# Normalised x turned into matrix operands by transfers and a VectorE block transpose instead of TensorE transposes

## The chip, the cores and the metric

The kernel runs on one core of a Trainium2 chip. The core has TensorE (PE in the profile; its weight loads are PEld), VectorE (DVE), ScalarE (ACT), GpSimd (POOL) and SyncE (SP), which here issues every DMA. SBUF is the on-chip memory with 128 partitions, PSUM the accumulators that TensorE writes. The metric is the device time of one execution in microseconds; the time of a kernel is the median of its runs.

## The reference

The input x is 8 x 2048 x 512 in fp32. Two layers with a residual each. The second is a layer with 16 experts that take `s_len // 16` tokens each; its sequence length here is 8, so each takes none, and what is left of it is a layer norm with gain and shift. The first layer is where the change lies:

```python
x = x + _layernorm(_L0_attn_ref(_layernorm(x, axis=-1), Wq, bq, Wk, bk, Wv, bv, Wo, bo), axis=-1)
x = x + _layernorm(_L0_ffn_ref(_layernorm(x, axis=-1), ...), axis=-1)

def _L0_attn_ref(x, Wq, bq, Wk, bk, Wv, bv, Wo, bo):
    n, s, e = x.shape
    h, d = (16, 32)
    def proj(W, b):
        y = jnp.einsum('nse,fe->nsf', x, W) + b
        return y.reshape(n, s, h, d).transpose(0, 2, 1, 3)
    Q, K, V = proj(Wq, bq), proj(Wk, bk), proj(Wv, bv)
    scores = jnp.einsum('nqhd,nkhd->nhqk', Q, K) * scale
    attn = jax.nn.softmax(scores, axis=-1)
    out = jnp.einsum('nhql,nlhd->nqhd', attn, V)
    out = out.reshape(n, s, e)
    return jnp.einsum('nse,fe->nsf', out, Wo) + bo
```

`proj` hands over (n, head, position, d), and the einsums name the second axis q, k or l and the third h: for every token this is attention among its own 16 heads. The result, with the head outermost, is reshaped straight into rows.

## The kernel before

**Tiling.** The 16,384 tokens are cut into 32 units of 512 tokens, and a unit into four tiles of 128. A unit goes through four steps, c = 0 to 3. Everything is fp32 and the order of all instructions is written out by hand (`manual_schedule`): each engine, and the SP queue, runs its instructions in the order in which the program issues them.

**What a step holds.** `STEPS[c]` is a string of items that `step` walks through. While step (u, c) does the softmax and the weighing of unit u, it also computes part of the products for Q, K and V of unit u + 1 (items such as `q1`, `k5`, with `e` for the copy out of PSUM and `w` for the write to a DRAM scratch), the output product and row work of unit u - 1 (`d1` to `d7`, `ra` to `re`), and prepares the x tile s + 8 or s + 9, where s = 4u + c. The products use Strassen's scheme: seven products of quarters (`multiply`, line 317) instead of eight, so x is needed also as sums and differences of its quarters.

**The path of an x tile before the change.** `load_x` (line 243) loads tile s + 11 in step s (item `lx`), one token per partition. `stat_x` and `norm_x` (items `xs`, `xn`, tile s + 9; lines 183, 190, 191, 260, 261) subtract the mean and multiply by the inverse deviation on VectorE, with the inverse root on POOL, and POOL's memset puts a 1 in the last column (for the biases). One step later, for tile s + 8, `turn_x` (item `px`, line 267) turns the tile with four 128 x 128 TensorE transposes into one PSUM bank, so that features lie on partitions. `keep_x` (item `xa`, lines 279 and 281) copies it with ACT into `xb`, the operands of a unit (seven quarter blocks of 2 x 256 columns). For the tiles 2 and 3 of a unit `add_x` (item `xt`) makes t3 and t1 on VectorE (lines 290, 291; one source is the PSUM bank) and t2 and t4 on POOL (lines 292, 293).

Feature `128*ec + p` lies in chunk ec on partition p, and the weights for Q, K and V are loaded in the same order (`load_weight`, line 139, `"(ec p) f -> p ec f"`).

**TensorE around it.** In steps 1, 2 and 3 `px` stands at the end of the step, ahead of the scores of the next step (`sc`, line 393) and the weighing of this one (`av`, line 442). In step 0 it stands at the beginning, ahead of the product `q1` (tile `paq`).

**SP.** In the order of the items: x and r loads (`lx`, `lr`), writes of Q, K and V to DRAM (lines 364, 367; `qs<-cq`, `ks<-ck`, `vs<-cv`), their spreads back in another layout (`sq`, `sk`: line 376, `qd<-qs`, `kx<-ks`; `sv`: line 382, `vd<-vs`) and stores of finished rows (`st`, line 589). A DMA that has to wait for its data holds up those behind it. `kx` and `vd` have one buffer each. Step 2 ends in `k3w sc av` and step 3 begins with `sk lx lr`; the scores that need that `kx` are issued at the end of step 3.

**VectorE and the softmax.** Each step begins its softmax with `mx` (lines 404, 406: the maximum and the subtraction), then ACT's exp (414), the sum and reciprocal (419, 420), POOL's product (421), a VectorE block transpose of 32 x 32 blocks (426), and four ACT copies into `ex` (431), which the weighing reads.

**The start.** `first_unit` prepares tiles 0 to 7, all weights and the products of unit 0 in an order of its own; `FIRST_STEPS` replaces `STEPS` in unit 0. The last two units have no x tiles left to prepare.

Of the kernel before, what the change touches and what calls it, by code (L numbers as in the profile page):

```python
# [34 lines left out]
F32 = mybir.dt.float32  # L35
BF16 = mybir.dt.bfloat16
AF = mybir.ActivationFunctionType
ALU = mybir.AluOpType
# [12 lines left out]
def head_attention_norms(  # L51
# [15 lines left out]
    nc = tc.nc  # L67
    NB, S, E = x.shape
    P = 128
    H, D = 16, 32  # L70
    assert NB // H == 0, "experts that take tokens"
    EC = E // P
    Q4 = 4
# [3 lines left out]
    NT = Q4 * NU  # L77
    SCALE = 1.0 / D**0.5

    const = ctx.enter_context(tc.tile_pool(name="const", bufs=1))  # L80
    xpool = ctx.enter_context(tc.tile_pool(name="xpool", bufs=4))
    pool2 = ctx.enter_context(tc.tile_pool(name="pool2", bufs=2))
    epool = ctx.enter_context(tc.tile_pool(name="epool", bufs=2))
    dpool = ctx.enter_context(tc.tile_pool(name="dpool", bufs=4))
# [4 lines left out]
    ps_pj = ctx.enter_context(tc.tile_pool(name="ps_pj", bufs=4, space=PSUM))  # L89


    ident = const.tile([P, P], F32, name="ident")
# [43 lines left out]

    def load_weight(name, src, last=False):
        weights[name] = w = const.tile([P, EC, E], F32, name="w" + name)
        src = src.rearrange("(ec p) f -> p ec f", p=P)
        if not last:  # L140
            nc.sync.dma_start(w, src)
            return
        sums[name] = epool.tile([P, E], F32, tag="cc", name="last" + name, bufs=6)
        nc.sync.dma_start(sums[name], src[P - 1 : P, EC - 1, :].to_broadcast([P, E]))
        for i in range(2):
            nc.sync.dma_start(w[:, 2 * i : 2 * i + 2, :], src[:, 2 * i : 2 * i + 2, :])
# [27 lines left out]
    def load_row(name, b):  # L174
        t = const.tile([P, E], F32, name="r" + name)
        nc.sync.dma_start(t, b.unsqueeze(0).to_broadcast([P, E]))
        row_const[name] = t
# [59 lines left out]
    xs, xrs, xb, px = {}, {}, {}, {}  # L237

    def load_x(t):
        if t < NT:  # L240
            xs[t] = xpool.tile([P, E], F32, tag="x", name=f"x_{t}")
            n, s = divmod(P * t, S)
            nc.sync.dma_start(xs[t], x[n, s : s + P, :] if t < NT - Q4 else renumbered[t % Q4])

    def renumber(J):

# [3 lines left out]
    renumbered = dram.tile([Q4, P, E], F32, tag="xr", name="xr", bufs=1)  # L250

    def stat_x(t):
        if t < NT:
            mv = moments(xs[t], f"x{t}")
            xrs[t] = mv, rsqrt(mv[:, 1:2], f"x{t}", 1.0, EPS)

    def norm_x(t):
        if t < NT:
            mv, rs = xrs.pop(t)
            nc.vector.tensor_scalar(xs[t], xs[t], mv[:, 0:1], rs, ALU.subtract, ALU.mult)  # L260
            nc.gpsimd.memset(xs[t][:, E - 1 : E], 1.0)

    def turn_x(t):
        if t < NT:
            px[t] = ps_pj.tile([P, EC, P], F32, tag="pj", name=f"px_{t}")
            for ec in range(EC):
                nc.tensor.transpose(px[t][:, ec, :], xs[t][:, ec * P : (ec + 1) * P], ident)  # L267
            del xs[t]

    def keep_x(t):  # L270

        if t < NT:
            u, J = divmod(t, Q4)
            if J == 0:
                xb[u] = pool2.tile([P, 7, 2, 2 * P], F32, tag="xb", name=f"xb_{u}")
            j = slice(P * (J % 2), P * (J % 2) + P)
            if J < 2:
                dst = xb[u][:, 0:2].rearrange("p n e t -> p (n e) t")[:, :, j]
                nc.scalar.copy(dst, px[t])
            else:  # L280
                nc.scalar.copy(xb[u][:, 2, :, j], px[t][:, 2:4])  # L281

    def add_x(t):

        if t < NT and t % Q4 >= 2:
            u, J = divmod(t, Q4)
            j = slice(P * (J % 2), P * (J % 2) + P)
            b11, b21, b22, t1, t2, t3, t4 = (xb[u][:, n, :, j] for n in range(7))
            b12 = px[t][:, 0:2]
            nc.vector.tensor_tensor(t3, b22, b12, ALU.subtract)  # L290
            nc.vector.tensor_tensor(t1, b12, b11, ALU.subtract)
            nc.gpsimd.tensor_tensor(t2, b22, t1, ALU.subtract)
            nc.gpsimd.tensor_tensor(t4, b21, t2, ALU.subtract)

# [5 lines left out]
    def multiply(u, name, n):  # L300
        if n == 1:
            banks[name, "a"] = ps_a.tile([P, E], F32, tag="pa", name=f"pa{name}_{u}")
        elif n in (2, 5):
            banks[name, n] = ps_pj.tile([P, E], F32, tag="pj", name=f"p{name}{n}_{u}")
        ps = banks[name, {2: 2, 5: 5, 3: 5}.get(n, "a")]
        w, t = weights[name], sums[name]
        lo, hi = slice(0, 256), slice(256, 512)
        left = {
            1: w[:, 0:2, lo], 2: w[:, 2:4, lo], 3: w[:, 0:2, hi], 4: w[:, 2:4, hi],
            5: t[:, 0], 6: t[:, 1], 7: t[:, 2],  # L310
        }[n]
        right = xb[u][:, {1: 0, 2: 1, 3: 2, 4: 6, 5: 3, 6: 4, 7: 5}[n]]
        if name == "v":
            left, right = right, left
        for m in range(2):
            for e in range(2):
                nc.tensor.matmul(  # L317
                    ps[:, 256 * m : 256 * m + 256],
                    lhsT=left[:, e, P * m : P * m + P], rhs=right[:, e, :],
                    start=(n in (1, 2, 5) and m == 0 and e == 0), stop=(e == 1), skip_group_check=True,  # L320
                )
# [275 lines left out]
    def first_unit():  # L597
# [12 lines left out]
        stat_x(0)  # L610
        stat_x(1)
        norm_x(0)
        turn_x(0)
        keep_x(0)
        stat_x(2)
        norm_x(1)
        turn_x(1)
        keep_x(1)
        stat_x(3)
        norm_x(2)  # L620
        turn_x(2)
        keep_x(2)
        norm_x(3)
        turn_x(3)
        keep_x(3)
        for t in range(4, 8):
            load_x(t)
        load_weight("v", wvT, True)
# [18 lines left out]
        add_weights("k", nc.vector, (1,))  # L647
        run(0, "q3 k6 k6e q4w q5w q3e k2e")
        norm_x(4)
        stat_x(5)  # L650
        add_weights("v", nc.gpsimd)
        run(0, "q3w")
        spread_qk(0, "q")
        run(0, "k2w k5 k7 k7e v1 v1e k4 k5e k4e")
        norm_x(5)
        run(0, "k3 k4w k5w k3e k3w")
        spread_qk(0, "k")
        stat_x(6)
        run(0, "v2 v2e v2w v6 v6e")
        turn_x(4)  # L660
        keep_x(4)
        norm_x(6)
        turn_x(5)
        stat_x(7)
        load_x(8)
        run(0, "v7 v7e")
        keep_x(5)
        load_x(9)
        norm_x(7)
        turn_x(6)  # L670
        keep_x(6)
        load_x(10)
        add_x(6)
        turn_x(7)
        keep_x(7)
        run(0, "v5 v4 v5e v4e v4w v5w")
        stat_x(8)
        add_x(7)
        run(0, "v3 v3e v3w")
        scores(0, 0)  # L680
        norm_x(8)

    def run(u, items):

        for item in items.split():
            f = {"": multiply, "e": collect, "w": write}.get(item[2:])
            if f:
                f(u, item[0], int(item[1]))
# [1 line left out]


    STEPS = (
        "lx lr sv st ok sB px mx xa q1 q1e ra d2 ou dn d2e rv d6 d6e tr d5 x0 x1 x2 x3 d7 d7e rg rf q2 rt d5e xs"
        " d4 q2e re xn d4e d3 d3e rs q2w st sc av",
        "lx lr q6 q6e mx ra dn ok ou q5 rv q7 tr q7e x0 x1 x2 x3 k1 rg rf q5e k1e rt q4 xs q3 q4e re k2 q3e xn"
        " q5w q4w rs px st xa q3w k2e sc av",
        "lx lr k6 k6e mx ra dn ok ou k5 rv k7 tr k7e k2w x0 x1 x2 x3 v1 sq rg k5e rf v1e rt k4 xs k4e k5w k3 re xn"
        " k3e k4w rs px st xa xt k3w sc av",
        "sk lx lr v2 mx v2e ra v6 ok v6e dn ou ds v5 rv sA v7 tr x0 x1 v7e x2 x3 d1 rg rf v5e v2w d1e v4 rt xs"
        " v4e v5w v3 re xn v3e v4w rs px xa xt v3w sc av",  # L700
    )

    FIRST_STEPS = (
        "lx sv mx q1 q1e dn ok ou q2 q2e q6 q6e tr k1 k1e x0 x1 x2 x3 q7 q7e q2w lb xs q5 q5e xn q4 q4e px q5w q4w lo"
        " xa sc av",
        "lx k2 mx k2e dn ok ou c4 q3 tr k6 k6e x0 x1 x2 x3 q3e k2w q3w k5 xs cs k7 k7e c0 k5e xn px k5w xa sc av",
        "lx mx v1 v1e dn ok ou k4 k4e k3 k3e tr k4w k3w sq c1 v2 x0 x1 x2 x3 v2e xs c2 c3 v6 v6e xn wt px xa xt v2w sc av",
        "sk lx ds v7 v7e mx v5 v5e dn ok ou xs tr v4 v4e xn x0 x1 x2 x3 d1 sA v4w v5w d1e px v3 v3e xa xt v3w lg sc av",
    )
    stores = []  # L710

    def step(u, c):
        s = Q4 * u + c
# [7 lines left out]
        def keep_last():  # L721
# [6 lines left out]
            "x0": lambda: soft_place(0), "x1": lambda: soft_place(1),  # L728
            "x2": lambda: soft_place(2), "x3": lambda: soft_place(3),
            "av": lambda: weigh(u, c), "ok": keep_last, "ou": lay_under, "sq": lambda: spread_qk(u + 1, "q"), "sk": lambda: spread_qk(u + 1, "k"), "st": store,  # L730
            "xs": lambda: stat_x(s + 9), "xn": lambda: norm_x(s + 9), "px": lambda: turn_x(s + 8),
            "lb": lambda: load_row("o", bo), "lo": lambda: load_weight("o", woT), "lg": load_gains,
            "c0": lambda: centre_output(0), "c1": lambda: centre_output(1), "c2": lambda: centre_output(2),
            "c3": lambda: centre_output(3), "c4": lambda: centre_output(Q4), "cs": split_bias, "wt": add_output,
            "xa": lambda: keep_x(s + 8), "xt": lambda: add_x(s + 8),
        }
        of_last = {
            "ra": lambda: rows_add(*d), "rv": lambda: rows_var(*d), "rg": lambda: rows_gain(*d),
# [139 lines left out]
```

## Time and profile before

| what | value |
| --- | --- |
| median of 3 runs | 1885.67 us (1885.27 to 1886.52) |
| span of the profiled execution, first to last instruction | 1882.1 us |
| DMA packets, bytes | 370,051 packets, 312.58 MB |
| q1 hardware queue, share of the 16 engines' span | 63.0% |
| transposes of x on PE (line 267) | 512, 281 ns mean |
| copies px to xb on ACT (lines 279, 281) | 64 of 595 ns and 64 of 503 ns mean |
| subtractions on VectorE (lines 290, 291) | 64 of 417 ns and 64 of 423 ns mean |
| a unit (four steps) | 57.2 us |

The time of the profiled execution itself is not recorded apart from its span; the median of the runs is 3.6 us longer than the span. A group line of the profile gives the line of the program, the engine, the operation, what it writes and reads with shapes, how often, then the busy time, the mean duration in ns, and the idle time of the engine just before such instructions with what ended it.

### The profile page before, as it was taken

To read this page: it belongs to the slowest core of one execution; us is meant where nothing else is said; L and a number is where in the kernel's file an instruction comes from. 1 tells how busy PE (TensorE), PEld (TensorE's weight loads), DVE (VectorE), ACT (ScalarE), POOL (GpSimd) and SP (SyncE) were. 2 spreads that over 40 slices of the span, in tenths; PEclk is the share of its full clock that TensorE was granted. 3 is DMA by queue.
4 is the path that set the end of the run, shared out by engine and by line. 5 is a ranking of instruction groups with operands and counts; after the bars stand their busy time and mean duration, and the time that the engine had idled before them with its cause. 6 is when DMAs were issued, how large, how long until landed. Compare 5 with 4: busy or idle time off the path is not lost.

```text
span 1882.1 us, 57927 instructions
## 1 busy us (share of the span) xinstructions
PE 1847.4 (98%) x24026; PEld 1596.9 (85%) x24026; DVE 1423.8 (76%) x2634; ACT 1172.4 (62%) x1910; POOL 1028.9 (55%) x1785
## 2 busy tenths in 40 slices
PE   8999999999999999999999999999999999999994
PEld 7888888888888888888888888888888888888872
DVE  7667777777777777777777777777777777777777
ACT  2556566666666665666666666566666656666666
POOL 5345654555554565555556545555545555455546
PEclk9999999999999999999999999999999999999998
DMA  7765766566766657665667665576556677656671
GB/s 218 187 158 154 186 174 162 152 167 166 181 169 161 166 147 191 175 162 150 171 157 185 172 163 161 154 181 180 161 158 168 157 189 193 165 147 163 154 186 57
DMA packets 370051, 312.58 MB, mean 166 GB/s; under 512 B 149750, under 2 KB 280825, under 8 KB 365564
## 3 DMA queue, kind: packets, MB, share of 16 engines
q1 hardware_dynamic: 369788, 308.89, 63.0%
q8 instruction: 188, 3.08, 0.7%
q14 instruction: 75, 0.61, 0.1%
HBM read 174.59 MB, written 135.27 MB: 165 GB/s over the span
## 4 chain that ended last, share of the span: by engine, by line
PE 93%; POOL 2%; DVE 1%; ACT 1%; DMA 1%; issue 1%; SPq 0%; POOLq 0%; ACTq 0%; DVEq 0%
PE paq L317 12%; PE pak L317 12%; PE pav L317 11%; PE pad L507 11%; PE pk L317 9%; PE pq L317 9%; PE pv L317 9%; PE pd L507 8%; PE sa L393 6%; PE sa L442 4%; PE px L267 3%; ACT ex L431 1%; POOL rs_d L191 1%; POOL e L421 0%; POOL rs_d L190 0%
## 5 line engine op out<-in xcount | busy, mean ns | idle before, releaser
L431 ACT COPY ex<-eT 32x512 f32<-32x512 f32 x512 | 315.5, 616 | 40.1 <-DVE eT L426 31.2
L421 POOL TENSOR_TENSOR e<-e,den 128x512 f32<-128x512 f32 x128 | 134.6, 1052 | 323.2 <-DVE den L420 265.4
L191 POOL TENSOR_TENSOR rs_d<-rs_d,nhalf 128x1 f32<-128x1 f32 x384 | 211.1, 550 | 32.0
L588 POOL TENSOR_TENSOR a<-a,r 128x512 f32<-128x512 f32 x120 | 181.7, 1514 | 44.1 <-ACT a L584 27.0
L190 POOL TENSOR_SCALAR rs_d<-mv_d 128x1 f32<-128x1 f32 x250 | 50.1, 200 | 255.9 <-DVE mv_d L184 242.8
L404 DVE TENSOR_REDUCE top<-sa 128x16 f32<-128x512 f32 x128 | 88.7, 693 | 103.5 <-PE sa L442 66.7
L584 ACT ACTIVATE a<-a,nm,rs_d 128x512 f32<-128x512 f32 x120 | 97.7, 814 | 97.2 <-DVE nm L577 97.2
L414 ACT ACTIVATE e<-e 128x512 f32<-128x512 f32 x128 | 80.8, 631 | 122.7 <-DVE e L406 122.5
L453 ACT COPY oT<-sa 128x512 f32<-128x512 f32 x124 | 134.4, 1084 | 31.8 <-PE sa L442 29.6
L260 DVE TENSOR_SCALAR x<-x,mv_x,rs_x 128x512 f32<-128x512 f32 x128 | 94.7, 740 | 53.5 <-POOL rs_x L191 52.8
L419 DVE TENSOR_REDUCE den<-e 128x16 f32<-128x512 f32 x128 | 87.2, 681 | 62.9 <-ACT e L414 62.8
L393 PEld LDWEIGHTS sa<-kx,qd 64*32 64x32 f32 x8192 | 109.2, 139 | 29.9 <-issue 27.7
L133 ACT COPY sa<-under 128x1024 f32<-128x1024 f32 x129 | 131.7, 1021 | 2.1
L426 DVE STREAM_TRANSPOSE eT<-e 128x512 f32<-128x512 f32 x128 | 91.0, 711 | 54.7 <-POOL e L421 54.7
L393 PE MATMUL sa<-kx,qd 64*32 64x64 f32 x8192 | 129.1, 249 | 1.0 <-DMA vs<-cv 0.9
L543 ACT ACTIVATE junk<-a 128x512 f32<-128x512 f32 x120 | 84.1, 701 | 71.7 <-DVE a L521 71.7
L442 PE MATMUL sa<-ex,vd 64*32 64x64 f32 x8192 | 123.2, 226 | 3.9 <-ACT ex L431 3.4
L317 PE MATMUL paq<-xb,sq 128*128 128x256 f32 x512 | 124.2, 386 | 0.1
L317 PE MATMUL pak<-xb,sk 128*128 128x256 f32 x512 | 124.2, 386 | 0.0
L317 PE MATMUL pv<-wv,xb 128*128 128x256 f32 x512 | 124.1, 385 | 0.0
L317 PE MATMUL paq<-xb,wq 128*128 128x256 f32 x512 | 123.2, 384 | 0.7 <-ACT xb L281 0.4
L317 PE MATMUL pav<-wv,xb 128*128 128x256 f32 x512 | 121.2, 380 | 1.0 <-ACT u3v L337 1.0
(163 smaller groups left out, 4719.8 us busy)
## 6 DMA issues: line engine op xcount, KB each, us to landing
qs<-cq SPq DMA_DIRECT2D x128, 256.0 KB, 2.3
qd<-qs SPq DMA_DIRECT2D x128, 256.0 KB, 5.3
ks<-ck SPq DMA_DIRECT2D x128, 256.0 KB, 2.4
kx<-ks SPq DMA_DIRECT2D x128, 256.0 KB, 4.3
vs<-cv SPq DMA_DIRECT2D x128, 256.0 KB, 3.1
vd<-vs SPq DMA_DIRECT2D x128, 256.0 KB, 4.4
r<-in_x_dram SPq DMA_DIRECT2D x128, 256.0 KB, 4.9
x<-in_x_dram SPq DMA_DIRECT2D x124, 256.0 KB, 4.5
```

The lines of the kernel that those rows point to most:

```text
L133: nc.scalar.copy(sa, under.unsqueeze(1).to_broadcast([P, 2, UT]))
L191: nc.gpsimd.tensor_tensor(rs, rs, nhalf, ALU.pow)
L260: nc.vector.tensor_scalar(xs[t], xs[t], mv[:, 0:1], rs, ALU.subtract, ALU.mult)
L317: nc.tensor.matmul(ps[:, 256 * m : 256 * m + 256], lhsT=left[:, e, P * m : P * m + P], rhs=right[:, e, :], start=(n in (1, 2, 5) and m == ...
L393: nc.tensor.matmul(sa[32 * i : 32 * i + 32, t, 64 * rh : 64 * rh + 64], lhsT=qd[u][d].rearrange("p h (b m) -> p (h b) m", b=2)[:, :, m], r ...
L421: nc.gpsimd.tensor_tensor(e, e, den.unsqueeze(2).to_broadcast([P, 16, 32]), ALU.mult)
L431: nc.scalar.copy(ex[q, :, i % 2, :], sm["t"][q])
L442: nc.tensor.matmul(o[:, J], lhsT=vd[u][d, 4 * c + rh, J, :], rhs=ex[d, 8 * (J // 2) + 2 * rh + J % 2].rearrange("p i k -> p (i k)"), start ...
L453: nc.scalar.copy(dst, sa[:, :, 256:].rearrange("p t (k h R) -> p t k h R", k=Q4, h=Q4))
L507: nc.tensor.matmul(ps[:, m], lhsT=left[:, e, P * m : P * m + P], rhs=right[:, e], start=(n in (2, 5) and m == 0 and e == 0), stop=(e == 1) ...
L584: nc.scalar.activation(a, a, AF.Identity, bias=nm, scale=rs)
L588: engine.tensor_tensor(a, a, res.pop((u, k)), ALU.add)
```

## The change

Tiles 0 to 3 are turned on TensorE as before, but with a stride of four, so that chunk k holds the features 4p + k. From tile 4 on another path is taken:

- `load_x` loads a tile so that partition 4t + b holds token 32b + t.
- `move_x` (new item `xm`, tile s + 9, near the end of the step) issues four SBUF-to-SBUF transfers on SP. Transfer a takes columns 128a to 128a + 127 of all 128 partitions and lays them into the 32 partitions from 32a on: partition 32a + t then holds, for b = 0 to 3, the 128 columns of token 32b + t.
- `turn_x` (item `px`, now one place ahead of `xn`) is one VectorE transpose of 32 x 32 blocks that reads the moved tile with a stride of four elements and writes the operands in `xb` directly. The item `xa`, ACT's copy, is gone.
- `add_x` reads its third quarter from `xb` and writes t1 over it; the numbers of the blocks change accordingly.
- The weights for Q, K and V are loaded with their rows in order 4p + k.
- `xpool` has five buffers instead of four, `mpool` (two buffers) is new, and `dynamic_dma_scratch_size` is set to 1024.

```diff
-    xpool = ctx.enter_context(tc.tile_pool(name="xpool", bufs=4))
+    xpool = ctx.enter_context(tc.tile_pool(name="xpool", bufs=5))
+    mpool = ctx.enter_context(tc.tile_pool(name="mpool", bufs=2))
...
-        src = src.rearrange("(ec p) f -> p ec f", p=P)
+        src = src.rearrange("(p ec) f -> p ec f" if last else "(ec p) f -> p ec f", p=P)
...
-            nc.sync.dma_start(xs[t], x[n, s : s + P, :] if t < NT - Q4 else renumbered[t % Q4])
+            src = x[n, s : s + P, :] if t < NT - Q4 else renumbered[t % Q4]
+            nc.sync.dma_start(xs[t], src if t < Q4 else src.rearrange("(b t) e -> t b e", b=Q4))
...
+    def begin_x(t):
+        u, J = divmod(t, Q4)
+        if J == 0:
+            xb[u] = pool2.tile([P, 7, 2, 2 * P], F32, tag="xb", name=f"xb_{u}")
+        j = slice(P * (J % 2), P * (J % 2) + P)
+        n = 0 if J < 2 else 2
+        return xb[u][:, n : n + 2].rearrange("p n e t -> p (n e) t")[:, :, j]
+
+    def turn_first(t):
+        px[t] = ps_pj.tile([P, EC, P], F32, tag="pj", name=f"px_{t}")
+        for ec in range(EC):
+            part = xs[t].rearrange("p (e k) -> p k e", k=EC)[:, ec]
+            nc.tensor.transpose(px[t][:, ec, :], part, ident)
+        del xs[t]
+
+    def keep_first(t):
+        nc.scalar.copy(begin_x(t), px.pop(t))
+
+    def move_x(t):
+
+        if t < NT:
+            px[t] = mpool.tile([P, Q4, P], F32, tag="xm", name=f"xm_{t}")
+            for a in range(Q4):
+                nc.sync.dma_start(px[t][32 * a : 32 * a + 32], xs[t][:, P * a : P * a + P])
+            del xs[t]
+
     def turn_x(t):
+
         if t < NT:
-            px[t] = ps_pj.tile([P, EC, P], F32, tag="pj", name=f"px_{t}")
-            for ec in range(EC):
-                nc.tensor.transpose(px[t][:, ec, :], xs[t][:, ec * P : (ec + 1) * P], ident)
-            del xs[t]
-
-    def keep_x(t):
...
+            dst = begin_x(t).rearrange("p k (b t) -> p k b t", b=Q4)
+            nc.vector.transpose(dst, px.pop(t).rearrange("p b (e k) -> p k b e", k=EC))
...
-            b11, b21, b22, t1, t2, t3, t4 = (xb[u][:, n, :, j] for n in range(7))
-            b12 = px[t][:, 0:2]
-            nc.vector.tensor_tensor(t3, b22, b12, ALU.subtract)
-            nc.vector.tensor_tensor(t1, b12, b11, ALU.subtract)
+            b11, b21, t1, b22, t2, t3, t4 = (xb[u][:, n, :, j] for n in range(7))
+            nc.vector.tensor_tensor(t3, b22, t1, ALU.subtract)
+            nc.vector.tensor_tensor(t1, t1, b11, ALU.subtract)
...
-        right = xb[u][:, {1: 0, 2: 1, 3: 2, 4: 6, 5: 3, 6: 4, 7: 5}[n]]
+        right = xb[u][:, {1: 0, 2: 1, 3: 3, 4: 6, 5: 2, 6: 4, 7: 5}[n]]
...
     STEPS = (
-        "lx lr sv st ok sB px mx xa q1 q1e ra d2 ou dn d2e rv d6 d6e tr d5 x0 x1 x2 x3 d7 d7e rg rf q2 rt d5e xs"
-        " d4 q2e re xn d4e d3 d3e rs q2w st sc av",
-        "lx lr q6 q6e mx ra dn ok ou q5 rv q7 tr q7e x0 x1 x2 x3 k1 rg rf q5e k1e rt q4 xs q3 q4e re k2 q3e xn"
-        " q5w q4w rs px st xa q3w k2e sc av",
-        "lx lr k6 k6e mx ra dn ok ou k5 rv k7 tr k7e k2w x0 x1 x2 x3 v1 sq rg k5e rf v1e rt k4 xs k4e k5w k3 re xn"
-        " k3e k4w rs px st xa xt k3w sc av",
+        "lx lr sv st ok sB mx q1 q1e ra d2 ou dn d2e rv d6 d6e tr d5 x0 x1 x2 x3 d7 d7e rg rf q2 rt d5e xs"
+        " d4 q2e re px xn d4e d3 d3e rs q2w st xm sc av",
+        "lx lr q6 q6e mx ra dn ok ou q5 rv q7 tr q7e x0 x1 x2 x3 k1 rg rf q5e k1e rt q4 xs q3 q4e re k2 q3e px xn"
+        " q5w q4w rs st q3w xm k2e sc av",
+        "lx lr k6 k6e mx ra dn ok ou k5 rv k7 tr k7e k2w x0 x1 x2 x3 v1 sq rg k5e rf v1e rt k4 xs k4e k5w k3 re px xn"
+        " k3e k4w rs xt st k3w xm sc av",
         "sk lx lr v2 mx v2e ra v6 ok v6e dn ou ds v5 rv sA v7 tr x0 x1 v7e x2 x3 d1 rg rf v5e v2w d1e v4 rt xs"
-        " v4e v5w v3 re xn v3e v4w rs px xa xt v3w sc av",
+        " v4e v5w v3 re px xn v3e v4w rs xt v3w xm sc av",
     )
...
-    nc = _bacc.Bacc("TRN2", target_bir_lowering=False, num_devices=1)
+    nc = _bacc.Bacc("TRN2", target_bir_lowering=False, num_devices=1, dynamic_dma_scratch_size=1024)
```

In `first_unit` and `FIRST_STEPS` the items move in the same way: `turn_first` and `keep_first` for tiles 0 to 3, `move_x` after `norm_x` for tiles 4 to 8, `turn_x` where the TensorE transposes of tiles 4 to 7 stood or a little later.

## Prediction

> **What bounds the kernel.** I read the page first: busy time, the slices, the chain that ended last. Then the busy time by stage, then the chain in order of time over one unit.
>
> ```profile
> span 1882.1 us, 57927 instructions
> ...
> PE 1847.4 (98%) x24026; PEld 1596.9 (85%) x24026; DVE 1423.8 (76%) x2634; ACT 1172.4 (62%) x1910; POOL 1028.9 (55%) x1785
> ...
> PEclk9999999999999999999999999999999999999998
> ...
> PE 93%; POOL 2%; DVE 1%; ACT 1%; DMA 1%; issue 1%; SPq 0%; POOLq 0%; ACTq 0%; DVEq 0%
> ```
>
> ```profile
> 900.00:1300.00 400.00, 399.97 (x5262) 349.79 (x5261) 307.21 (x574) 254.25 (x413) 220.62 (x385) 1.00 0.64 167
> ```
>
> In the second fence (busy PE, PEld, DVE, ACT, POOL, then clock, DMA share, GB/s) PE is busy 399.97 of 400 us, at the full granted clock, and nothing interrupts it. Between 100 and 1700 us, 28 units of 57.2 us, it is busy 1598.11 of 1600. So work taken off PE shortens the span, as long as nothing else becomes late.
>
> **What the transposes cost PE.** Their own durations (281 ns x 512 = 144 us) overlap, so I take the chain's steps instead (start, length, what):
>
> ```profile
> 905.78 0.59 PE px L267 x4
> 906.37 1.73 PE paq L317 x8
> ...
> 918.48 1.73 PE pd L507 x8
> 920.20 0.89 PE sa L393 x50
> 921.10 0.71 PE sa L442 x46
> 921.81 1.92 PE paq L317 x8
> ...
> 932.37 1.73 PE pk L317 x8
> 934.09 0.44 PE px L267 x4
> 934.53 0.88 PE sa L393 x52
> ```
>
> Steps 1, 2 and 3 of a unit have four transposes ahead of the scores: 0.44 us, and the scores take 0.88 with them or 0.89 without. In step 0 they stand behind the weighing: 0.59 us, but the product behind them takes 1.73 instead of 1.92, so they are worth 0.40. A unit: 3 x 0.44 + 0.40 = 1.72 us. Tiles 8 to 127 fill 30 units: **51.6 us**. The first unit's tiles 4 to 7 take 2 x 0.87 = 1.7 us in the chain; I count these apart below. If the next instructions did not speed up or slow down at all, the bound above is 0.53 us a tile (start of the first transpose at 933.93 to the scores at 934.46): 120 x 0.53 + 1.7 = 65 us.
>
> **ACT.** 124 copies of px go (about half of 595 ns, half of 503): some 68 us off an engine at 62%. It is not the bound, so it is worth nothing by itself.
>
> **VectorE.** Added per tile: one block transpose. The trace has one of the same size.
>
> ```profile
> L404 DVE TENSOR_REDUCE top<-sa 128x16 f32<-128x512 f32 x128 | 88.7, 693 | 103.5 <-PE sa L442 66.7
> L260 DVE TENSOR_SCALAR x<-x,mv_x,rs_x 128x512 f32<-128x512 f32 x128 | 94.7, 740 | 53.5 <-POOL rs_x L191 52.8
> L426 DVE STREAM_TRANSPOSE eT<-e 128x512 f32<-128x512 f32 x128 | 91.0, 711 | 54.7 <-POOL e L421 54.7
> L453 ACT COPY oT<-sa 128x512 f32<-128x512 f32 x124 | 134.4, 1084 | 31.8 <-PE sa L442 29.6
> ```
>
> L426 reads and writes in order: 0.71 us is the lower bound. The new one reads every fourth element. No VectorE row does that; the nearest is L453, an ACT copy that writes every eighth element and takes 1084 ns where in-order ACT copies of that size (L331) take 585, 1.85 times. 0.711 x 1.85 = 1.32 us is the upper bound; adding the same 0.50 us gives 1.21. Against it, VectorE's write of every second element (ck, L353, 684 ns) costs no more than one in order (cq, 683). I take 1.2. The Trainium skill, Vector Engine (DVE) Microarchitecture Reference, section Measured stream behaviour on trn2, says that a stream runs at full rate only in runs of two adjacent words, and lists 1.73 to 2.5 ns per column where every element hops. By it the transpose would take about 1.1 to 1.5 us, an estimate from 512 columns and the page's two prices, and the sum below would hardly move; the ck row, whose hop of one word is free, doesn't follow that rule.
>
> The two subtractions of add_x now read SBUF twice instead of SBUF and PSUM. Nearest are L552 and L566, SBUF alone: 0.74 us as a rule and 1.03 when a POOL add runs beside them. Half as wide, that is 0 to 0.15 us each, four per unit; I take 0.14, so 0.56. (Once, in the start, an SBUF add beside POOL took 2.73 us instead of 0.69; that is the bound above, 1.0 us each.)
>
> Is there room? Between 100 and 1700 us VectorE waits, per unit, 3.30 us for the scores ahead of L404 (58.2 + 34.1 over 28), 0.95 for pd, 0.56 for pq, 0.47 for pv: 5.28 us in which it stands early for PE. Another 1.78 (49.9 over 28) is spent ahead of norm_x's subtraction for POOL's rsqrt, and the new transpose is issued just before that, so it fills this gap. Need: 4 x 1.2 + 0.56 + 1.72 (PE is sooner) - 1.78 = 5.3 us. So the early arrival is just used up. Behind it stand 2.01 us of waits for ACT's exp and 0.82 for ACT's copy, part of which shrink when VectorE is later, and in every step ex is ready 2 to 4 us before the weighing takes it (step 2: 944.93, weighing from 947.7). I cost it at nothing; without the early arrival, 5.36 - 1.78 = 3.6 us a unit, 107 us in 30, would be on the path.
>
> **SP and DMA.** 124 x 4 = 496 issues of 64 KB. Issues of the spreads take 0.43 us, so 1.7 us per tile; SP waits 1080 of the 1600 us, so it has the time. The order matters.
>
> ```profile
> 949.66 1.14 SPq L367 DMA_DIRECT2D ks<-ck  x1
> 950.90 3.19 SPq L376 DMA_DIRECT2D kx<-ks  x4
> ```
>
> The tightest place: in step 2 the last write of K (949.66), then now the move, then the spread of K that the scores at 961.4 need. Two of the four spreads wait for that write to land anyway (34.7 us over 28 units, 1.24 us each; qs and ks land in 2.3). The move's 1.7 us mostly fill that. Its packets (512, each 512 bytes, like qs<-cq) cost 16 engines 51 ns a packet on the mean (63.0% of 16 x 1882.1 us over 369,788): 1.6 us. The last spread lands at 953.7 + 4.2 = 957.9; with PE sooner by two transposes' 0.88 the scores want it at 960.5. Slack 2.6 us, needed 0.5 + 1.6 = 2.1. What waits behind the move on SP otherwise (loads for one and two steps on, the spread of V, which lands at 914.3 for a weighing at 920.2) has 4 us or more. The move waits for norm_x and the POOL memset, for which SP's store before it already waits (L589 on x L261, 123 us in the stage). The moved tile has 8 to 10 us until its transpose; spreads land in 8.9 at the worst. In all DMA rises from 63% by about 11 points (63,488 packets x 51 ns over 16 engines, 203 us). x's rows fetched in another order cost what r's scattered rows do (4.9 us to landing, against 4.5), two steps ahead of use. A fifth x buffer makes up for a tile that is held until its move has landed instead of until PE has read it.
>
> The trap in the Trainium skill that speaks against this: VectorE: DVE Perf Modes, The three transpose paths, calls a plain strided DMA 19 times slower than the crossbar path (1309 ns), so about 25 us a block by estimate. It holds for a large stride in the innermost dimension; here 512-byte runs move, as in qs<-cq (2.3 us). By the rule each step would wait some 15 us for its tile (25 less the 8 to 10 above), 1800 us over 120 steps, and the sum would be above 3600. No run here shows the rule.
>
> **Start.** Scores and weighing of unit 0 hang on V's last part (cv ends 52.9, vs, vd lands 61.9). Tile 7's transpose and the subtractions now stand ahead of it on VectorE, with the wait for the move: about +0.8; one move and a load then stand ahead of the spread: +0.9. The end of that chain comes 1.7 us later, and the 1.7 us saved on PE there are lost too: -1.7 net. Tiles 0 to 3 stay on PE, read with a stride: weight loads with a stride (L393) take 139 ns, in order (L442) 106, so 16 x 0.03 = 0.5 us at most, taken as 0. q, k and v weights come in another row order, in longer pieces, and wait as little as before. dynamic_dma_scratch_size: POOL issues no DMA here, nothing. The last eight steps and the last unit have no x work.
>
> **Sum.** 51.6 - 1.7 = 49.9; 1882.1 - 49.9 = 1832.2 of span. The runs' median is 3.6 above the span: **1835.8, say 1836 us**.
>
> **Rivals.**
> - *Full gain* (forecast, 0.58): at most the 65 us of the upper PE price, at least 40 (a third of a microsecond of late scores per unit): 1821 to 1846.
> - *VectorE becomes the bound* (0.18): transpose 1.32 us, subtractions 0.4 each: 5.28 + 1.6 + 1.72 - 1.78 = 6.8 against 5.28; 1.5 us a unit, 46 us in 30, so 1882. Half of it is taken up by ACT's waits: 1859. For: 76% becomes 86%. Against: the 2.8 us of other waits.
> - *K arrives late* (slower, 0.19): SP's order. If none of the move's issue hides (+1.7), its packets take twice as long in the stretch where the DMA share is already 1.0 (+3.2), and the transpose delays the last K sum by 0.5: 5.4 against 2.6 us of slack, 2.8 a unit, 84 us in 30: 1836 + 84 = 1920. It decides from 1.7 us late per unit on. For: DMA is full from 952 to 962 us. Against: the landing wait already there.
> - *The transposes were hidden*, or what PE saves is lost again at the next wait (0.05): 1885. Against: PE 93% of the chain, px 3% by name.
>
> **From this**: about 0.2% (4 us) is what can be told from no change. Faster 0.58 + 0.18 = 0.76, same 0.05, slower 0.19. The range holds the first two, up to where VectorE takes nearly all: 1821 to 1884; the forecast's own is 1821 to 1846.
>
> **What would show it.** Right: px gone from PE after 12 us, scores following a product directly, units of 55.5 us, PE still over 399 of 400, L426-like transposes near 1.2 us, the wait before L404 near zero. Wrong: idle PE ahead of L393 released by a kx or ks DMA (K late) or ahead of L442 by ex (VectorE late); transposes over 1.6 us; a move that lands over 8 us after issue.

## Result and profile after

| | before | after |
|---|---|---|
| median of the runs (us) | 1885.47 (1883.57 to 1886.52, 4 runs) | **1928.8** (1924.4 to 1929.94, 4 runs) |
| profiled span (us) | 1882.1 | 1922.6 |
| unit, most frequent length (us) | 57.21 | 58.33 |
| start of unit 1 on TensorE (us) | 104.27 | 111.33 |

The ratio is 1.0227, with a 95% interval of 1.0213 to 1.0242. The changed kernel is 2.3% slower; 1836 us were forecast, and the result lies outside the range.

From the page of the changed kernel, the busy times, the chain that ended last and three groups of instructions:

```profile
span 1922.6 us, 57824 instructions
...
PE 1821.5 (95%) x23530; PEld 1535.4 (80%) x23530; DVE 1602.6 (83%) x2758; ACT 1122.4 (58%) x1786; POOL 1035.2 (54%) x1785
...
PE 47%; DVE 14%; DMA 12%; POOL 12%; issue 7%; SPq 5%; ACT 3%; DVEq 0%; POOLq 0%; ACTq 0%
...
L295 DVE STREAM_TRANSPOSE xb<-xm 128x512 f32<-128x512 f32 x124 | 160.2, 1292 | 7.4 <-DMA xm<-x 6.3
L520 PE MATMUL pad<-so,oS 128*128 128x256 f32 x480 | 120.9, 385 | 42.0 <-POOL oS L490 42.0
...
L262 DVE TENSOR_SCALAR x<-x,mv_x,rs_x 128x512 f32<-128x512 f32 x128 | 143.5, 1121 | 1.8 <-POOL rs_x L192 1.1
```

The chain fell from 93% TensorE to 47%, and VectorE and POOL have 14% and 12% of it. TensorE now waits for POOL ahead of the output product `pad` (the row's third part: 42.0 us, put down to `oS`); before, that wait was 0.2 us. norm_x (L262, before L260) lost its wait of 52.8 us for POOL's inverse root, but its own busy time rose from 94.7 to 143.5 us. The new transposes take 1292 ns. The same stretch as before, by stage (busy PE, PEld, DVE, ACT, POOL, then clock, DMA share, GB/s):

```profile
900.00:1300.00 400.00, 386.40 (x4996) 328.97 (x4995) 341.92 (x590) 238.50 (x376) 218.83 (x377) 1.00 0.70 183
```

TensorE, busy 399.97 of 400 us before, now idles 13.6; its clock is still 1.00.

**One wait, followed back.** The timeline of one change from step 3 to step 0 in the changed kernel (start, length, engine, what), first VectorE, then POOL, then TensorE:

```profile
924.69 1.52 DVE L295 STREAM_TRANSPOSE xb<-xm 128x512 f32<-128x512 f32 x1
926.15 1.33 DVE L262 TENSOR_SCALAR x<-x,mv_x,rs_x 128x512 f32<-128x512 f32 x1
927.39 0.68 DVE L366 TENSOR_TENSOR cv<-pv,u2v 128x512 f32<-128x512 f32 x1
928.00 0.41 DVE L303 TENSOR_TENSOR xb<-xb 128x256 f32<-128x256 f32 x1
928.44 0.42 DVE L304 TENSOR_TENSOR xb<-xb 128x256 f32<-128x256 f32 x1
```

```profile
925.92 1.27 POOL L601 TENSOR_TENSOR a<-a,r 128x512 f32<-128x512 f32 x1 [0.54 <-ACT a L597]
...
928.95 0.72 POOL L305 TENSOR_TENSOR xb<-xb 128x256 f32<-128x256 f32 x1
929.75 0.73 POOL L306 TENSOR_TENSOR xb<-xb 128x256 f32<-128x256 f32 x1
930.43 1.17 POOL L489 TENSOR_TENSOR oS<-oT 128x256 f32<-128x256 f32 x1
931.68 0.72 POOL L490 TENSOR_TENSOR oS<-oS,oT 128x256 f32<-128x256 f32 x1
```

```profile
930.06 0.59 PE L520 MATMUL pad<-so,oS 128*128 128x256 f32 x2
932.46 1.56 PE L520 MATMUL pad<-so,oS 128*128 128x256 f32 x6 [1.81 <-POOL oS L490]
```

The same place in the kernel before, VectorE and POOL:

```profile
903.71 0.55 DVE L260 TENSOR_SCALAR x<-x,mv_x,rs_x 128x512 f32<-128x512 f32 x1 [0.75 <-POOL rs_x L191]
...
905.35 0.42 DVE L291 TENSOR_TENSOR xb<-px,xb 128x256 f32<-128x256 f32 x1
```

```profile
903.89 1.79 POOL L588 TENSOR_TENSOR a<-a,r 128x512 f32<-128x512 f32 x1 [0.21 <-ACT a L584]
...
906.59 0.73 POOL L292 TENSOR_TENSOR xb<-xb 128x256 f32<-128x256 f32 x1
907.40 0.72 POOL L293 TENSOR_TENSOR xb<-xb 128x256 f32<-128x256 f32 x1
908.09 0.73 POOL L476 TENSOR_TENSOR oS<-oT 128x256 f32<-128x256 f32 x1
908.89 1.06 POOL L477 TENSOR_TENSOR oS<-oS,oT 128x256 f32<-128x256 f32 x1
```

In both, POOL makes t2 and t4 of x (L305 and L306, before L292 and L293) ahead of the sums of the weighed values `oS` (L489 and L490, before L476 and L477), and `pad` needs the second of these. The product `pd` before it starts at 907.93 before and at 928.33 after. Measured from there, VectorE's last subtraction ends 2.2 us early before (905.77) and 0.5 us late after (928.86), a loss of 2.7 us; POOL's `oS` is done at +2.0 before (909.95), just as `pad` takes it, and at +4.1 after (932.40). From this come the 1.81 us for which TensorE stands. The transpose of 1.52 us and norm_x's 1.33 are where VectorE loses the time. Norm_x meets POOL's add of `a` in both kernels. Before, norm_x begins first (903.71) and takes 0.55 us, and the add (903.89) takes 1.79. After, the add begins first (925.92) and takes 1.27, and norm_x (926.15) takes 1.33. POOL's own queue is late as well: t2 (L305) starts 0.09 us after the last subtraction and 0.14 after POOL's instruction before it, where in the kernel before add_x had been ready for 0.8 us when POOL came to t2.

### The profile page after: what moved, and what is told of

It is laid out like the page before. It is cut to its first block, busy times and chain, and to the rows that moved or that the text cites. A ratio compares the mean times of both kernels' runs of the same rounds, so it can differ in the third digit from the quotient of the medians.

```text
span 1922.6 us, 57824 instructions
## 1 busy us (share of the span) xinstructions
PE 1821.5 (95%) x23530; PEld 1535.4 (80%) x23530; DVE 1602.6 (83%) x2758; ACT 1122.4 (58%) x1786; POOL 1035.2 (54%) x1785
## 4 chain that ended last, share of the span: by engine, by line
PE 47%; DVE 14%; DMA 12%; POOL 12%; issue 7%; SPq 5%; ACT 3%; DVEq 0%; POOLq 0%; ACTq 0%
PE paq L330 9%; PE pq L330 8%; PE pad L520 8%; PE pak L330 6%; PE pd L520 6%; DMA r<-in_x_dram 4%; DVE x L262 4%; DMA qd<-qs 4%; PE pk L330 3%; PE sa L406 3%; PE sa L455 2%; POOL oS L489 2%; SPq L288 2%; POOL oS L490 2%; SPq L389 2%
## 5 line engine op out<-in xcount | busy, mean ns | idle before, releaser
L192 POOL TENSOR_TENSOR rs_d<-rs_d,nhalf 128x1 f32<-128x1 f32 x384 | 226.8, 591 | 32.0
L601 POOL TENSOR_TENSOR a<-a,r 128x512 f32<-128x512 f32 x120 | 161.8, 1348 | 52.8 <-ACT a L597 52.8
L597 ACT ACTIVATE a<-a,nm,rs_d 128x512 f32<-128x512 f32 x120 | 106.2, 885 | 110.5 <-DVE nm L590 110.5
L295 DVE STREAM_TRANSPOSE xb<-xm 128x512 f32<-128x512 f32 x124 | 160.2, 1292 | 7.4 <-DMA xm<-x 6.3
L520 PE MATMUL pad<-so,oS 128*128 128x256 f32 x480 | 120.9, 385 | 42.0 <-POOL oS L490 42.0
L262 DVE TENSOR_SCALAR x<-x,mv_x,rs_x 128x512 f32<-128x512 f32 x128 | 143.5, 1121 | 1.8 <-POOL rs_x L192 1.1
L520 PEld LDWEIGHTS pad<-so,oS 128*128 128x128 f32 x480 | 88.9, 190 | 64.2 <-POOL oS L490 53.3
L330 PE MATMUL paq<-xb,wq 128*128 128x256 f32 x512 | 127.3, 392 | 2.6 <-issue 1.6
```

The costliest lines, as they stand in the source:

```text
L192: nc.gpsimd.tensor_tensor(rs, rs, nhalf, ALU.pow)
L295: nc.vector.transpose(dst, px.pop(t).rearrange("p b (e k) -> p k b e", k=EC))
L330: nc.tensor.matmul(ps[:, 256 * m : 256 * m + 256], lhsT=left[:, e, P * m : P * m + P], rhs=right[:, e, :], start=(n in (1, 2, 5) and m == ...
L520: nc.tensor.matmul(ps[:, m], lhsT=left[:, e, P * m : P * m + P], rhs=right[:, e], start=(n in (2, 5) and m == 0 and e == 0), stop=(e == 1) ...
L601: engine.tensor_tensor(a, a, res.pop((u, k)), ALU.add)
```

## Experiments

Theory A is the chain just read: VectorE has too much to do ahead of add_x, POOL's queue stands behind add_x, and `pad` behind that. Theory B is that the transfers cost the time. Times are medians beside the kernel before on the same chip (1884.3 to 1886.6). PE idle is what is missing to 1600 us of busy TensorE between 100 and 1700 us of the profiled execution; it shows only part of what the units lose (28 units of the changed kernel take 75 us more than 28 of e10, but PE idle is 53 us more). e1 to e7 ran once each, e9 to e11 twice, e8 four times and e12 five times. The runs of one kernel lie up to 5.5 us apart for the changed kernel and 11.3 us for e12, so a few microseconds between single runs tell nothing. e2, e9 and e10 leave the transfers out and so compute another output; they are there for their time alone.

| run | time (us) | unit, most frequent (mean) | PE idle |
|---|---|---|---|
| before | 1885.47 | 57.21 | 1.9 |
| after | 1928.8 | 58.33 (58.38) | 58.7 |
| e1 before + transfers | 1898.26 | 57.21 (57.75) | 10.1 |
| e2 after, no transfers | 1915.53 | 58.30 | 55.9 |
| e3 features in order | 1904.51 | (57.53) | 43.4 |
| e4 late sums | 1879.08 | 56.4 (56.82) | 21.2 |
| e5 norm_x first | 1915.92 | 57.7 (58.07) | 51.6 |
| e6 in order + late sums | 1873.64 | (56.67) | 25.4 |
| e7 late sums + start on TensorE | 1881.19 | 56.4 (57.10) | 22.8 |
| e8 all three | 1866.8 | 55.5 to 56.5 (56.57) | 21.7 |
| e9 late sums, no transfers | 1861.59 | 56.4 (56.38) | 8.6 |
| e10 all three, no transfers | 1841.15 | 55.5 (55.71) | 5.6 |
| e11 before + extra transpose | 1918.73 | 58.4 (58.45) | 24.0 |
| e12 e8, K's spread first | **1846.09** | 55.5 (55.84) | 10.2 |

**Transfers or VectorE (e1, e2).** e1 adds the four transfers per tile to the kernel before, from unit 1 on, at their new places, into a tile that nobody reads. e2 takes them out of the changed kernel.

```diff
 e1, on the kernel before
+            xm = mpool.tile([P, Q4, P], F32, tag="xm", name=f"xm_{t}")
+            for a in range(Q4):
+                nc.sync.dma_start(xm[32 * a : 32 * a + 32], xs[t][:, P * a : P * a + P])
 e2, on the kernel after
-            px[t] = mpool.tile([P, Q4, P], F32, tag="xm", name=f"xm_{t}")
-            for a in range(Q4):
-                nc.sync.dma_start(px[t][32 * a : 32 * a + 32], xs[t][:, P * a : P * a + P])
-            del xs[t]
+            px[t] = xs.pop(t).rearrange("p (b e) -> p b e", b=Q4)
```

> The kernel before, with TensorE's transposes, to which only the four transfers per tile are added on SP at the changed kernel's places, into a tile that nobody reads. Theory A (VectorE has too much to do in steps 2 and 3, add_x is late, POOL's sums for the output product are late, TensorE waits 1.8 us in step 0): no change, 1882 to 1892 us. Theory B (the transfers hold up K's spread or other DMAs): 1905 us or more, TensorE idle ahead of the scores with a DMA as releaser.

> The changed kernel without the four transfers: the block transpose reads the normalised tile itself, so tokens and features of the operands are mixed up and the output is another one. Theory A: as the changed kernel, 1915 to 1932 us. Theory B: the transfers were what held it up, 1850 us or less.

e1 took 1898.26 us, some 12 more than before and between the two expectations: half of the units keep 57.2 us, and the others take up to 61. e2 took 1915.53, in A's range: without any transfer nearly all of the loss is still there, and with it the wait (the groups of the page of e2):

```profile
L517 PE MATMUL pad<-so,oS 128*128 128x256 f32 x480 | 121.2, 385 | 51.3 <-POOL oS L487 51.3
```

So the regular 58.3 us per unit don't come from the transfers; what they cost by themselves is smaller: irregular delays in e1, and in the changed kernel mostly the start (unit 1 begins at 104.43 us in e2, at 111.33 with the transfers).

**The stride (e3).** Features go in order (chunk a, then k, then 32 in a row), so that the transpose reads runs of 32 elements; the weights' rows follow, loaded in four pieces of 32 partitions.

```diff
-            nc.vector.transpose(dst, px.pop(t).rearrange("p b (e k) -> p k b e", k=EC))
+            nc.vector.transpose(dst, px.pop(t).rearrange("p b (k e) -> p k b e", k=EC))
```

> The changed kernel with features in order 128a + 32k + e, so that the block transpose reads its source in runs of 32 elements instead of every fourth; the weights' rows are loaded to match, and tiles 0 to 3 are normalised into that order. The transpose should take 0.7 to 0.9 us instead of 1.29. Theory A: VectorE gains about 2 us a unit, 1.2 to 1.6 of it in steps 2 and 3, so 36 to 48 us less than 1929: 1880 to 1893 us. Theory B: 1925 to 1932 us.

1904.51 us: 24 better than the changed kernel, but A asked for 1880 to 1893. The groups of the page of e3:

```profile
L526 PE MATMUL pad<-so,oS 128*128 128x256 f32 x480 | 119.7, 384 | 18.2 <-POOL oS L496 18.0
L301 DVE STREAM_TRANSPOSE xb<-xm 128x512 f32<-128x512 f32 x124 | 90.5, 730 | 10.3 <-DMA xm<-x 8.9 <-DMA r<-in_x_dram 0.4
...
L267 DVE TENSOR_SCALAR x<-x,mv_x,rs_x 128x512 f32<-128x512 f32 x124 | 81.2, 655 | 2.6 <-POOL rs_x L192 1.8
L309 DVE TENSOR_TENSOR xb<-xb 128x256 f32<-128x256 f32 x64 | 58.0, 906 | 0.0
```

The transpose falls from 1292 to 730 ns and norm_x from 1121 to 655, and the wait for `oS` is more than halved. But now it is add_x's first subtraction (L309, 906 ns against some 0.42 us before) that meets POOL's add. And unit 1 starts at 117.7 us, 6.4 later than in the changed kernel, which I put down to the weights, loaded in pieces (e6, where they load as before the change, begins unit 1 at 111.2).

**The queue on POOL (e4).** For the unit's last tile, t2 and t4 are taken out of POOL's queue ahead of `oS` and put behind the product of the softmax in the next step.

```diff
+            if late and t % Q4 == 3:
+                return
+    def add_rest(t):
...
             nc.gpsimd.tensor_tensor(t2, b22, t1, ALU.subtract)
             nc.gpsimd.tensor_tensor(t4, b21, t2, ALU.subtract)
...
-" d2e rv d6 d6e tr"
+" d2e rv d6 d6e xp tr"
```

> The changed kernel with POOL's two subtractions (t2, t4) of a unit's last tile put behind the softmax's product in the next step 0, so that POOL's sums for the output product do not stand behind add_x. Theory A with the POOL queue as the path: TensorE's 1.8 us wait per unit goes, 45 to 54 us less: 1875 to 1885 us. Theory A with VectorE itself as the bound whatever POOL does: the wait turns up elsewhere, 1905 to 1930 us. Theory B: unchanged, 1925 to 1932 us.

1879.08 us, as A expected: VectorE works as slowly as before (transposes 1286 ns, norm_x 1138), and yet 50 us are gone. The group of the page of e4 that had waited 42.0 us:

```profile
L530 PE MATMUL pad<-so,oS 128*128 128x256 f32 x480 | 113.4, 379 | 0.0
```

Two POOL instructions in another place settle what the path was. The kernel is now faster than the one before, by some 7 us in its one run.

**The filled gap (e5).** norm_x ahead of the transpose again.

```diff
-re px xn
+re xn px
```

> The changed kernel with norm_x's subtraction again ahead of the block transpose (items xn px instead of px xn). In the changed kernel the subtraction comes 1.3 us later than before, meets POOL's add L601 and takes 1.18 us instead of 0.75. If that meeting is what eats the gap that the transpose was to fill: the subtraction goes back to 0.7 to 0.8 us, VectorE's wait for rsqrt (about 0.4 us a tile) comes back, and the time stays within 8 us of 1929. If the order was well chosen: 10 us or more slower than 1929. If the meeting costs more than the gap: 1905 to 1918 us.

1915.92 us, 13 less than the changed kernel, as the third case of the expectation has it. The groups of the page of e5:

```profile
L295 DVE STREAM_TRANSPOSE xb<-xm 128x512 f32<-128x512 f32 x124 | 145.2, 1171 | 6.0 <-DMA xm<-x 6.0
...
L262 DVE TENSOR_SCALAR x<-x,mv_x,rs_x 128x512 f32<-128x512 f32 x128 | 102.5, 801 | 53.6 <-POOL rs_x L192 52.9 <-POOL x L263 0.7
```

The gap of 52.9 us is back, and the kernel is faster with it: norm_x takes 102.5 us instead of 143.5, and the transposes 145.2 instead of 160.2. Between 100 and 1700 us norm_x meets POOL's add of `a` about as often as in the changed kernel, but in 54 meetings it begins ahead of the add (0.71 us on the mean) and only in 27 behind it (1.31). In the changed kernel it begins behind the add in all 80 (1.42).

**Parts put together (e6 to e8).** e6 is late sums and features in order, with the weights' rows put in order ahead of the launch, so that they load as before the change; e7 late sums with tiles 4 to 7 of the start on TensorE; e8 all three.

> Both the in-order block transpose (0.73 us) and the late POOL sums; the rows of the Q, K and V weights are put into the order 128a + 32k + e ahead of the launch, so that they load as in the kernel before. Theory A: VectorE is no longer late, a unit takes 55.5 to 56.0 us against 58.4 (changed) and 57.2 (before), 28 units: 34 to 48 us less than before, 7 of it lost in the start: 1845 to 1860 us. If something else of the change holds the steps (SP's order, the DMA load): units stay at 56.4 or more, 1872 to 1885 us.

> The late POOL sums (stride kept), and tiles 4 to 7 turned on TensorE as in the kernel before, so that the start has no transfers but tile 8's. If the transfers on SP's queue are what makes unit 1 begin 7.1 us later than before (111.3 against 104.3 us): unit 1 begins at 104 to 106 us and the time is 5 to 8 us below 1879. If VectorE's new work in the start is the cause: no change from 1879.

> In-order transpose, late POOL sums and TensorE for tiles 4 to 7 together. Theory A: what the prediction forecast, since VectorE then needs 0.56 us less per tile: units of 55.5 to 55.9 us, unit 1 from 105 us: 1838 to 1850 us. Theory B: 1870 us or more.

1873.64, 1881.19 and 1866.8 us (e8 against before: 0.99, interval 0.9878 to 0.9922). A's ranges for e6 and e8 were missed, by 14 and 17 us; e6 is in the other theory's, e8 in neither. e7 and e8 begin unit 1 at 105.4 and 105.9 us instead of 111.3, so the start's loss is found. They take both the transfers and VectorE's transposes out of the start; that it was the transfers follows from e2 (104.43), which keeps these transposes. In e7's total, for which 5 to 8 us less than e4 had been expected, nothing of it shows; e8 is 7 us below e6's one run. The shortest units of e6 and e8 are the 55.5 us that were forecast, but others take up to 60. That irregular part had to be explained.

**What is irregular (e9, e10).** e4 and e8 without the transfers, with e2's edit.

> Late sums (e4, 1879.1 us) without the four transfers per tile; the transpose reads the x tile itself, so tokens and features are mixed. Theory S: the stalls of PE that come irregularly, with no releaser in the profile, come from the transfers; then the units take e4's most frequent 56.4 us throughout instead of its mean of 56.8, and PE idles under 10 us between 100 and 1700 instead of 21: 1879 - 28 x 0.42 = 1867, so 1862 to 1870. Rival: they come from the late sums or the order of VectorE's work; then e4's time, 1876 to 1882, and the same 21 us idle.

> e8 (1866.8 us: features in order, late sums, tiles 4 to 7 on TensorE) without the four transfers per tile; tokens and features are mixed. Theory S: units of 55.5 us, the shortest in e8, throughout instead of its mean of 56.57: 1867 - 28 x 1.07 = 1837, so 1832 to 1845; that is the saving on TensorE that was forecast. Rival (what is left in e8 is VectorE's or POOL's lateness): 1858 or more.

1861.59 and 1841.15 us: 17.5 and 25.7 us less, of which 6.5 and 1.3 are the start (unit 1 from 105.0 and 104.6 us). e9 came out a little below its range, e10 within it; the rival is out. In e9 every unit takes 56.3 to 56.5 us, in e10 23 of 28 take 55.5 to 55.7. From e10, the stretch by stage (columns as above):

```profile
100.00:1700.00 1600.00, 1594.45 (x21130) 1382.17 (x21131) 1341.58 (x2455) 994.24 (x1574) 915.43 (x1571) 1.00 0.66 171
```

That is the forecast's saving on TensorE, with VectorE as busy as 84% of the stretch. It also shows what the stride costs beside the late sums: 0.9 us per unit (e9 against e10), spread over waits of 0.1 to 0.3 us in step 3.

**VectorE's work alone (e11).** The kernel before with one more strided transpose per tile, ahead of norm_x, into a tile that nobody reads.

```diff
+            nc.vector.transpose(z, xs[t].rearrange("p (b e k) -> p k b e", b=Q4, k=EC))
...
-re xn
+re pz xn
```

> The kernel before with one more VectorE block transpose per tile, with a step of four elements, just ahead of norm_x, into a tile that nobody reads; no transfers, TensorE turns x as before. Theory A (VectorE's added work is enough to make POOL's sums late, and the output product waits for them): 1892 to 1912, PE waits for oS over 15 us in all. Rival (the added work still fits into VectorE's waits, and the loss needs norm_x's meeting with POOL's add in the changed order): 1882 to 1888, wait for oS under 5 us.

1918.73 us, more than A's range allowed, and the rival's 1882 to 1888 is out: without a transfer, and with TensorE turning x as ever, the units take 58.4 us, 0.1 more than in the changed kernel. But the wait for `oS` is only 7.3 us, not the 15 that A had named. The groups of the page and the waits of TensorE in e11:

```profile
L261 DVE TENSOR_SCALAR x<-x,mv_x,rs_x 128x512 f32<-128x512 f32 x128 | 143.4, 1120 | 14.5 <-POOL rs_x L192 1.3 <-POOL x L262 0.7
L267 DVE STREAM_TRANSPOSE xz<-x 128x512 f32<-128x512 f32 x115 | 137.8, 1198 | 0.0
```

```profile
PE px L273 <- DVE x L261: 14.8, 27, 0.7
PE pad L513 <- POOL oS L483: 7.3, 27, 0.3
```

Here the late norm_x (1120 ns, as in the changed kernel) holds TensorE first at its transposes of x, which the changed kernel no longer has, and POOL's sums get a little of that time back. It is the same lateness taken at another place: here VectorE doesn't get one such transpose per tile and norm_x behind POOL's add done in time. By the starts of the products (medians of 28 units) a unit loses 0.52 us at `pad` and 0.54 between its last product and the first of the next unit, where these transposes stand; that is nearly all of its 1.2. Since norm_x is late here too, e11 doesn't tell the transpose's own length from norm_x's meeting with the add.

**The order on SP (e12).** e8 holds step 2's transfers on SP between the last write of K and K's spread. e12 issues them behind the spread.

```diff
-" k3e k4w rs xt st k3w xm sc av"
-"sk lx lr v2 mx
+" k3e k4w rs xt st k3w sc av"
+"sk xq lx lr v2 mx
```

> e8 with the transfers of step 2 issued behind K's spread at the beginning of step 3 instead of ahead of it, where they hold SP for some 3.3 us. Theory S1 (the order on SP makes K late; that is the rival 'K arrives late' in small): PE's waits for kx fall from 9.7 us to about the 2 us of e10, and the time from 1866.8 to 1857-1862 us; waits without a releaser stay near 13 us. Rival S2 (the DMA engines' load makes K late, whatever the order): 1863 to 1870, kx waits still 7 us or more.

1846.09 us, 20.7 less than e8, below the ranges of both theories and so a larger gain than S1 expected. SP's part of the timeline, e8 and then e12:

```profile
711.81 0.54 SPq L396 DMA_DIRECT2D ks<-ck  x1
712.40 3.11 SPq L294 DMA_DIRECT2D xm<-x  x4
715.63 1.95 SPq L405 DMA_DIRECT2D kx<-ks  x4
```

```profile
706.65 0.66 SPq L396 DMA_DIRECT2D ks<-ck  x1
708.78 2.13 SPq L405 DMA_DIRECT2D kx<-ks  x4
710.95 3.54 SPq L294 DMA_DIRECT2D xm<-x  x4
```

The spread is issued 2.1 us after the start of that write instead of 3.8, and lands in 4.2 us instead of 5.4 (medians), without the transfer's packets ahead of it. TensorE's waits for `kx` fell from 9.7 to 5.4 us (from 8 times to 2), those for which the profile shows no releaser from 13.3 to 3.7, and 2.4 us for `vd` are new. S1 had expected about 2 us for `kx`, and no change in the second kind. That it fell with the first says that K's lateness was behind most of them too, or the load at that place; the trace doesn't tell which. Against the kernel before the ratio is 0.9801 (0.9782 to 0.9821): this version beats both, and is 5 us from e10, which has no transfers at all. What is left to the forecast of 1836 us is the irregular part: the mean unit of e12 has 55.84 us, and 0.34 x 30 is 10 us. e10, with a mean of 55.71, has more than half of that without any transfer.

## Why the prediction was wrong

- **TensorE's saving: right.** 1.72 us per unit were read off the chain, units of 55.5 us forecast. Where nothing else is late (e10) units take 55.5.
- **VectorE, "I cost it at nothing": the step that failed.** The need of 5.3 us per unit was set against 5.28 of room. Two things were wrong. First the size. The transpose's 1.2 us became 1.29, and the subtractions cost some 0.1 instead of 0.56 in all; the miss is the gap "which the transpose fills". It was filled (the wait went from 52.8 to 1.1 us), but norm_x was pushed behind the start of POOL's wide add and its busy time rose by 48.8 us, nearly as much as was gained. The trace of before had shown this: L260's mean of 740 ns mixes three cases (between 100 and 1700 us). 29 executions are alone (0.55 us), 55 begin 0.18 us ahead of the add (0.57) and 28 behind it (1.31). The transpose puts 1.3 us into a wait of 0.4 us per tile, and in the changed kernel norm_x begins behind the add in all 80 meetings. I took the mean. With this, the need is 4 x 1.29 + 0.1 + 1.72 - 1.78 + 4 x 0.38 = 6.7 us, 1.4 over the room. By that alone the unit would still have been shorter than before, 57.21 - 1.72 + 1.4 = 56.9 us (an estimate from these numbers), so this is only half of the miss.
- Second, the place. The room was added up over a unit, as if early time in one step served another. What counted was add_x in step 3, and behind it POOL's queue, of which the prediction says nothing: t2, t4 and `oS` were just in time before. VectorE's 2.7 us there became 1.81 us on TensorE per unit, and small waits elsewhere. I had looked for what is late next among VectorE's own waits (exp, `ex`), not at the engine that reads its results.
- **In numbers:** units of 58.33 instead of 55.5 are 2.83 x 30 = 85 us, of which e4's late sums take back 1.9 per unit and features in order the other 0.9. The start cost 7.1 us instead of 1.7. 1836 + 85 + 5.4 = 1926, against 1928.8. The starts of the products say the same: of the 2.8 us by which a unit of the changed kernel is longer than one of e10, 2.05 are lost at `pad` and 0.74 in step 3 (medians of 28 units).
- **Start: mis-sized.** The wait of the subtractions for the move was taken as 0.8 us. VectorE stood 5.86 us for tile 6's move, with the last copies of V behind it. VectorE and SP at that point of the changed kernel:

```profile
53.17 1.08 DVE L295 STREAM_TRANSPOSE xb<-xm 128x512 f32<-128x512 f32 x1 [5.86 <-DMA xm<-x]
54.18 0.65 DVE L366 TENSOR_TENSOR cv<-pv,u3v 128x512 f32<-128x512 f32 x1
```

```profile
47.26 2.56 SPq L288 DMA_DIRECT2D xm<-x  x4
49.93 1.25 SPq L245 DMA_DIRECT2D x<-in_x_dram  x2
51.27 2.58 SPq L288 DMA_DIRECT2D xm<-x  x4
```

- **Rival "VectorE becomes the bound": right engine, wrong ceiling.** It stopped at 1882, since it let VectorE take the saving and no more. VectorE late by more than TensorE's saving makes the unit longer than before.
- **Rival "K arrives late", 1920: close in number, wrong in cause here.** In the changed kernel TensorE waits 6.5 us in all for `kx`. But its mechanism is real: the units of 58.33 us gave K time, and as soon as they were 55.5 (e8), SP's order cost 20.7 us. Issues took 0.60 us each, not 0.43, so the move holds SP for 2.5 us or more.
- **Transfers:** landing in 2.8 us (median, at most 7.8), as hoped; a DMA share of 0.69 instead of 0.64 in the stretch. But the writes of K, for whose landing 2.3 us had been reckoned, land in 5.2 (median). The slow strided transfer that was weighed as a trap doesn't appear with pieces of 512 bytes.
- **The signs** named beforehand did their work: TensorE at 386.40 of 400 us and units of 58.33 deny the forecast at first sight, but neither of the two places named for the wait (ahead of the scores, ahead of the weighing) was the one.

## What to carry to other kernels

When work moves to an engine that is not the bound, follow its results step by step to the next queue: the first instruction that another engine holds behind them, with its slack at that place, counts, and not the sum of idle time. Look at the spread of a duration before its mean is used, and ask what a filled gap pushes on, and behind what it is pushed. And after one bound is taken away, look again at the rivals that its slack had covered: here two POOL instructions, the order of features, the start and four transfers on SP turned 2.3% slower into 2.0% faster.

## What the runs showed of the hardware

- When norm_x (VectorE, SBUF alone) and POOL's 128 x 512 add of `a` overlap, the one that begins first is held up little or not at all, and the other takes 0.5 us longer or more. In the kernel before norm_x takes 0.57 us where it begins 0.18 us ahead (55 times), and the add then 1.77 instead of 1.27; where the add began first norm_x takes 1.31 (28 times), in the changed kernel 1.42 (80 times), and alone 0.51 to 0.55. In e5, where it begins 0.18 to 0.50 us ahead, it takes 0.71 on the mean. e3's subtraction L309 takes 0.94 us behind the same add. L303 in the changed kernel stays at 0.41, but the POOL instruction beside it has a single column.
- Instructions of VectorE that also read PSUM show no clear rule: beside that add L290 in the kernel before takes 0.42 us and `cv` in e5 0.66, but `cv` and `ck` in the kernel before take 0.91 and 0.93 where 0.68 to 0.72 is usual. Why is open.
- The 32 x 32 block transpose of 128 x 512 takes 0.70 to 0.76 us on the mean when it reads runs of 32 elements, and 1.04 to 1.53 in the changed kernel, where it reads every fourth. It is dearest in steps 2 and 3 of the changed kernel (1.5), but POOL beside it doesn't account for that: 27 that run wholly beside the add of `a` take 1.11, and what decides is open.
- Extra transfers can stall TensorE for up to some 3 us at irregular places in waits for which the profile names no releaser (e8: 13.3 us in all, e10: 3.5). They came with the transfers and most went with their place on SP; how they act is open.
